# A fused decoder kernel: the second key stage recorded in written order, its rotations put behind the next product's addition, and layer 0's rows loaded sooner and taken ahead of the context

## The chip, the core and the metric

The kernel is one launch on one core of a Trainium2 chip. A core has a matrix engine (TensorE, PE in the profile), a vector engine (VectorE, DVE), an activation engine (ScalarE, ACT), a general engine (GpSimd, POOL) and a synchronising engine (SyncE, SP) that here only issues DMA transfers. Each engine takes the instructions of its own queue; semaphores order the engines among each other. The metric is device time in microseconds for one execution; lower is better.

## The reference, cut to what matters

Two batches of 512 rows of width 1024 pass through four residual layers; a context of 1024 rows per batch feeds the first and the third.

```python
x = x + matmul(fake_quant(layernorm(x)), fake_quant(ctx))           # layer 0 "xattn"
x = x + linear(layernorm(x)) + lora(...)                            # layer 0 "ffn"
x = x + attention(layernorm(x), ctx, ctx, mask, wq, wk, wv, wo)     # layer 1, rotated q and k
x = x + linear(layernorm(x)) + lora(...)                            # layer 1 "ffn"
# fake_quant: q = clip(round(x / scale + zp), 0, 255); (q - zp) * scale
# rope: x * cos + rotate_half(x) * sin
```

The keys `k = rope(ctx @ wk)` and the values `v = ctx @ wv` of layer 1 depend on the context alone, so the kernel makes them first; layer 0 is done beside them.

## The kernel before, in words

**Products.** Keys, values, queries and linear layers are multiplied in float32 as 2 by 2 blocks with seven products in place of eight. `seven` runs the products in the order 1, 2, 6, 7, 5, 4, 3. Its accumulators are the four PSUM banks of tag `b`; products 1 and 2 share a bank, 7 and 4, 5 and 3. A product that adds onto a shared bank can't begin until the earlier content has been read: product 4 waits for the addition L281, which reads product 7's bank, and product 3 waits for L283, which reads product 5's. Four products of 512 columns in 128-partition pieces make one `seven` product: eight matmul records of the trace, 3.4 to 3.5 us.

**Operands.** `right_steps` forms four sums of context blocks (L247, L250, L252, L255, each 128x2048) and `left_steps` four sums of weight blocks (L233, L236, L238, L241, each 128x1024), all on VectorE. Products 6, 7, 5, 4, 3 need them.

**Stages.** Keys come in two stages (`keys(0, 0, ...)` and `keys(0, 1, ...)`), each of two groups m = 0, 1 of seven products; then two value stages; then the same for batch 1. When a key block is complete, `emit` rotates it: `rope` calls `rope_steps`, two ScalarE copies of 64 partitions (L204, L205) and three VectorE operations (L207, L210, L211), and SP stores the result. In the first stage the order of TensorE, VectorE and ScalarE is the written one (`manual_schedule`). In the second stage and all that follows up to the attention, only TensorE keeps the written order; VectorE's and ScalarE's is made by a planner.

**Layer 0.** `quantized_product(b)` is a generator that `weave` advances once in two product steps. It first quantizes the eight blocks of context rows (L414 loads each, L182, L185, L186 quantize), then normalizes and quantizes four blocks of rows (`layernorm`, L151 to L156, then `quantized`), turns each on TensorE (L424), copies it out (`copy_out`, L144 on ScalarE and L146 on VectorE in turn), sums it (L427), and multiplies (L447, L461). The rows of batch 0 are loaded behind the first stage on ScalarE's DMA queue (L1119). Small operations on the quantization parameters (L1122 to L1126, `qp`) are written behind the first stage; the planner places them.

**Queues.** SP issues in order: the first weights and context blocks, rotation tables, the four quantization parameters (L1066), router weights (L1069) and gate weights (L1070); then key stores, later weights and context rows as they come.

**Attention.** A head's `exponential(j)` adds the negated maximum on VectorE (L809), takes the exponential on ScalarE (L812) and sums on GpSimd. While the first heads are filled in, the loop at L917 runs the last query products between them and calls `place_maximum` and `exponential` for the first head.

Of the kernel before, what the change touches and what calls it, by code (L numbers as in the profile page):

```python
# [39 lines left out]
def decoder_kernel(  # L40
# [139 lines left out]
    def quantized(dst, src, side):  # L180

        nc.vector.tensor_scalar(  # L182
            src, src, qp[f"{side}_inv"], qp[f"{side}_zp"], ALU.mult, ALU.add
        )
        nc.vector.tensor_scalar(src, src, 0.0, QMAX, ALU.max, ALU.min)  # L185
        nc.vector.tensor_scalar(dst, src, RND, RND + QMID, ALU.add, ALU.subtract)  # L186
# [6 lines left out]
        nc.scalar.copy(dsts[0], tr[:, 0:4, :])  # L193
        nc.vector.tensor_copy(dsts[1], tr[:, 4:8, :])

    def rope(dst, acc, half, scale):

        for _ in rope_steps(dst, acc, half, scale, nc.vector):
            pass

    def rope_steps(dst, acc, half, scale, eng):

        rot = u2([P, HALF])
        nc.scalar.activation(rot[0:64, :], acc[64:128, :], AF.Copy, scale=scale)  # L204
# [167 lines left out]
    def rows(b, t):  # L372
        return x[b][t // 2][:, t % 2, :]

    def halves():
        return [u8([P, 2, D]) for _ in range(2)]
# [30 lines left out]
        return right_sums(nc.vector, *quarters, lambda: u8([P, 4, HALF]))  # L407


    def quantized_product(b):  # L410
        q2 = [u8([P, 4, D], BF16) for _ in range(2)]
        for k in range(NKT):
            c_t = u4([P, D])
            nc.sync.dma_start(c_t, ctx_in[b, ts(k, P), :])  # L414
            quantized(q2[k // 4][:, k % 4, :], c_t, "x2")
            if k % 2:
                yield
        x1T = u8([P, NC, S], BF16)
        rsum, l1s = [], []

        def turned(t):
            tr = ps_wide().bitcast(BF16)[:, 0 : NC * P].rearrange("p (c n) -> p c n", c=NC)
            for c in range(NC):
                nc.tensor.transpose(tr[:, c, :], l1s[t][:, ts(c, P)], ident_b)  # L424
            copy_out(x1T[:, :, ts(t, P)], tr)
            r = small([P, 1])
            nc.scalar.activation(u4([P, D]), l1s[t], AF.Copy, accum_out=r)  # L427
            nc.vector.tensor_scalar(r, r, c_x2, None, ALU.mult)
            rsum.append(r)

        for t in range(NT):
            h = layernorm(rows(b, t))
            l1 = u2([P, D], BF16)
            quantized(l1, h, "x1")
            l1s.append(l1)
            if t > 1:
                turned(t - 2)
            yield
        turned(NT - 2)
        yield  # L440
        turned(NT - 1)
# [12 lines left out]
        csum = u4([P, D])  # L454
        nc.vector.tensor_scalar(csum, cs, kc2, c_x1, ALU.add, ALU.mult)
        yield
        for t in range(NT):
            acc = ps_wide()
            for n in range(2):
                for c in range(NC):  # L460
                    nc.tensor.matmul(  # L461
                        acc[:, ts(n, HALF)],
                        x1T[:, c, ts(t, P)],
                        q2[c // 4][:, c % 4, ts(n, HALF)],
                        start=(c == 0),
                        stop=(c == NC - 1),
                    )
            y = u4([P, D])
            nc.vector.scalar_tensor_tensor(y, acc, rsum[t], csum, ALU.add, ALU.add)
            xs = rows(b, t)  # L470
            nc.vector.scalar_tensor_tensor(xs, y, s12, xs, ALU.mult, ALU.add)
            yield


    def keys(b, q, ctx_ops, w, begun=(None, None)):
        def group(m):
            def product(i, acc, start):
                accumulate(
                    acc,
                    [(w[i - 1][:, c, ts(m, P)], ctx_ops[i - 1][:, c, :]) for c in range(4)],  # L480
                    start,
                )

            def emit(i, j, src):
                dst = u2([P, HALF]) if (i, j) == (0, 0) else src
                rope(dst, src, j, 1.0)
                nc.sync.dma_start(kT_d[b][4 * q + 2 * i + m][:, ts(j, HALF)], dst)

            return seven(product, emit, begun[m])

        return group(0), group(1)
# [359 lines left out]
    def attention(extra):  # L851
# [28 lines left out]
        for n in range(-2, total + GRP + 1):  # L880
# [36 lines left out]
            for i in range(extra.pop(n, 0)):  # L917
                for _ in range(2):
                    next(tree, None)
                next(extra["products"])  # L920

                if mid and not old and i == 1:
                    mid.place_maximum()
                    mid.exponential(0)
                if mid and not old and i == 2:
                    mid.exponential(1)
            if n == GRP:
                w_ops = {i: output_operand(0, i) for i in (1, 6, 2, 7, 5, 4, 3)}
            for _ in tree:
# [138 lines left out]
    nc.sync.dma_start(eb_t, ebias.partition_broadcast(P))  # L1068
    nc.sync.dma_start(r0_t, r0T.rearrange("(c p) e -> p c e", p=P))  # L1069
    nc.sync.dma_start(ga_t, gaT.rearrange("(c p) e -> p c e", p=P))  # L1070


    ctx_ops = [ctx_raw[0], ctx_raw[2]] + [None] * 5
# [2 lines left out]

    for i in range(20):
        nc.tensor.matmul(begun[0][:, :P], ones_b, ones_b, start=True, stop=True)
    first = [keys(0, 0, ctx_ops, w[0], begun), keys(0, 1, ctx_ops, w[1])]

    def layer_0():
        yield from quantized_product(0)
        put_away(0)
        x[1] = halves()
        load_rows(1, nc.sync)
        yield from quantized_product(1)

    with tc.manual_schedule(engines={mybir.EngineType.DVE, mybir.EngineType.Activation}):
# [13 lines left out]
        for g in first[0]:  # L1102
            next(g)
        next(first[0][0])
        next(rights)
        next(lefts)
        next(first[0][1])
        w[0][:] = next(lefts)
        ctx_ops[:] = next(rights)
        for _ in range(2):  # L1110
            for g in first[1]:
                next(g)
        lefts = left_steps(nc.vector, *wk_raw[1], lambda: u4([P, 4, 256]))
        for i, _ in enumerate(chain(*first[0])):
            if i in (4, 5, 6, 7):
                w[1][:] = next(lefts) or w[1]

        x[0] = halves()
        load_rows(0, nc.scalar)  # L1119

    for side in ("x1", "x2"):
        nc.vector.reciprocal(qp[f"{side}_inv"], qp[f"{side}_scale"])  # L1122
    for c_t, side in ((c_x1, "x1"), (c_x2, "x2")):
        nc.vector.tensor_scalar(c_t, qp[f"{side}_zp"], -1.0, QMID, ALU.mult, ALU.add)
# [3 lines left out]
    side = layer_0()  # L1128
    for b in range(B):
        if b == 1:  # L1130
            for ch in range(2):
# [3 lines left out]
        for i, stage in enumerate((keys, keys, values, values)):  # L1135
# [6 lines left out]
            if (b, i) == (0, 1):  # L1142
                main = chain(*first[1])
                raw = raw_weights(wv, 0)
                weave(main, side, 2)
                w = quad_sums(raw)
            else:
                main = pair(*stage(b, i % 2, ctx_ops, w))
                weave(main, side, 2)
                if i < 3:  # L1150
                    w = quad_weights((wk, wv)[(i + 1) // 2], (i + 1) % 2)
# [280 lines left out]
```

## Time and profile before

| What | us |
|---|---|
| median of 3 runs (lowest, highest) | 2435.92 (2434.83, 2436.45) |
| profiled execution, its own time | 2434.64 |
| its span | 2432.8 |
| TensorE busy | 2407.8 (99%) |
| VectorE busy | 1842.8 (76%) |
| GpSimd busy | 1024.5 (42%) |
| ScalarE busy | 527.2 (22%) |

Time is read in us from the start of the span. A bracket behind a row of the timeline names the idle time before it and what ended it. The stages that the diff touches lie in the first 205 us; one more edit lies near 955 us. In this trace TensorE starts the first key product at 3.92, the second key stage's remaining products after 68, the value products at about 111, and layer 0's products of batch 0 (L461) at 161.2.

### The profile page before, as it was taken

The numbers are of one execution on the slowest core, as the hardware profiler recorded it, in microseconds if no ns is written. First come the engines' busy times: TensorE is split into PE (matmuls) and PEld (weight loads), VectorE is DVE, ScalarE is ACT, GpSimd is POOL, SyncE is SP. The second block draws the span as 40 slices with busy tenths as digits, with TensorE's granted clock in tenths as the row PEclk, the third lists the DMA queues.
The fourth block names the chain that finished last, engine by engine and source line by source line (L and its number), as shares of the span: only waits on it lengthen the run. The fifth ranks groups of instructions, "written<-read, shape, count | busy, mean of one in ns | idle before, by whom it ended". The sixth has DMA issues, their size and how long they took to land.

```text
span 2432.8 us, 19529 instructions
## 1 busy us (share of the span) xinstructions
PE 2407.8 (99%) x6792; PEld 1195.1 (49%) x6792; DVE 1842.8 (76%) x1998; ACT 527.2 (22%) x623; POOL 1024.5 (42%) x543
## 2 busy tenths in 40 slices
PE   9999999999999999999999999999999999999999
PEld 4477458654444444444444444444444444444444
DVE  5849774345986556898888888888898988888753
ACT  1210221011222222322222222222223222222210
POOL 0000010210000002777676767667776767677531
PEclk9999999999999999999999999999999999999999
DMA  5437133013796221344223323442332243233501
GB/s 197 169 99 281 70 131 112 26 61 116 280 334 212 78 90 53 101 141 117 75 80 106 117 68 89 143 143 79 129 117 78 95 123 116 66 91 109 173 9 61
DMA packets 151506, 288.01 MB, mean 118 GB/s; under 512 B 32112, under 2 KB 49776, under 8 KB 149104
## 3 DMA queue, kind: packets, MB, share of 16 engines
q1 hardware_dynamic: 110880, 244.54, 30.6%
q10 hardware_dynamic: 40384, 41.70, 5.6%
q8 instruction: 54, 0.88, 0.1%
q0 software_dynamic: 144, 0.52, 0.1%
q14 instruction: 44, 0.36, 0.1%
HBM read 223.54 MB, written 63.18 MB: 118 GB/s over the span
## 4 chain that ended last, share of the span: by engine, by line
PE 55%; DVE 4%; issue 1%; POOL 0%; ACT 0%; POOLq 0%; DVEq 0%; ACTq 0%
PE b L345 20%; PE wide L763 16%; PE b L826 16%; PE wide L727 2%; DVE u L809 1%; DVE u L777 0%; DVE u L789 0%; DVE small L729 0%; DVE u L318 0%; DVE u L787 0%; PE b L967 0%; PE wide L192 0%; DVE u L791 0%; DVE u L785 0%; PE wide L1016 0%
## 5 line engine op out<-in xcount | busy, mean ns | idle before, releaser
L345 PE MATMUL b<-u,u 128*128 128x512 f32 (+1 forms) x3600 | 1384.5, 541 | 14.8 <-DVE u L283 4.2
L345 PEld LDWEIGHTS b<-u,u 128*128 128x128 f32 x3600 | 681.3, 191 | 684.0 <-issue 605.2
L826 PE MATMUL b<-u,u 128*128 128x512 f32 x1024 | 460.3, 592 | 0.0
L763 PE MATMUL wide<-u,u 128*128 128x512 f32 x1024 | 452.6, 593 | 2.6 <-DVE u L777 1.7
L815 POOL TENSOR_TENSOR u<-u 128x1024 f32<-128x1024 f32 x64 | 151.6, 2368 | 705.3 <-ACT u L812 696.8
L777 DVE TENSOR_TENSOR u<-wide,u 128x1024 f32<-128x1024 f32 x256 | 312.7, 1223 | 125.3 <-PE wide L763 125.1
L812 ACT ACTIVATE u<-u 128x2048 f32<-128x2048 f32 x128 | 244.7, 1911 | 665.1 <-DVE u L809 662.3
L763 PEld LDWEIGHTS wide<-u,u 128*128 128x128 f32 x1024 | 192.8, 190 | 250.9 <-issue 175.5
L809 DVE TENSOR_TENSOR u<-u,b 128x2048 f32<-128x2048 f32 x128 | 290.1, 2267 | 3.0 <-ACT b L805 3.0
L826 PEld LDWEIGHTS b<-u,u 128*128 128x128 f32 x1024 | 186.2, 192 | 184.6 <-issue 184.6
L300 POOL TENSOR_TENSOR u<-u,u 128x512 f32<-128x512 f32 x120 | 184.3, 1562 | 170.3 <-DVE u L312 134.6
L318 DVE TENSOR_TENSOR u<-u,b 128x512 f32<-128x512 f32 x200 | 135.6, 679 | 121.7 <-PE b L345 114.4
L818 POOL TENSOR_TENSOR u<-u,u 128x1024 f32<-128x1024 f32 x64 | 150.7, 2355 | 30.9 <-ACT u L812 30.7
L819 POOL TENSOR_TENSOR u<-u,u 128x1024 f32<-128x1024 f32 x64 | 150.8, 2356 | 5.0
L204 ACT ACTIVATE u<-u 64x512 f32<-64x512 f32 x72 | 45.2, 628 | 361.6 <-DVE u L283 162.5
L837 POOL TENSOR_TENSOR u<-u,u 128x512 f32<-128x512 f32 x64 | 115.0, 1797 | 18.4 <-DMA u<-row 18.4
L785 DVE TENSOR_TENSOR u<-u 128x1024 f32<-128x1024 f32 x64 | 113.0, 1765 | 0.0
L727 PEld LDWEIGHTS wide<-ident,u 128*128 128x128 f32 x512 | 79.9, 203 | 61.8 <-issue 55.7
L605 POOL TENSOR_TENSOR u<-u,u 128x1024 f32<-128x1024 f32 x8 | 20.2, 2528 | 213.0 <-DVE u L156 210.4
L787 DVE TENSOR_TENSOR u<-u,u 128x1024 f32<-128x1024 f32 x64 | 107.5, 1679 | 0.2
L820 POOL TENSOR_TENSOR u<-u 128x512 f32<-128x512 f32 x64 | 100.1, 1564 | 5.0
L1158 POOL DMA_DIRECT2D u<-in_b_dram x1 | 0.7, 717 | 229.1 <-PE b L345 229.1
(136 smaller groups left out, 1639.4 us busy)
## 6 DMA issues: line engine op xcount, KB each, us to landing
u<-row ACTq DMA_DIRECT2D x128, 256.0 KB, 3.5
u<-wo SPq DMA_DIRECT2D x64, 512.0 KB, 4.3
u<-in_wo_dram SPq DMA_DIRECT2D x48, 512.0 KB, 4.4
u<-in_wq_dram SPq DMA_DIRECT2D x32, 512.0 KB, 4.3
q<-u SPq DMA_DIRECT2D x64, 256.0 KB, 2.3
u<-in_wo_dram SPq DMA_DIRECT2D x16, 1024.0 KB, 8.0
wo<-u SPq DMA_DIRECT2D x32, 512.0 KB, 4.4
u<-q SPq DMA_DIRECT2D x64, 256.0 KB, 4.5
```

The costliest lines, as they stand in the source:

```text
L300: nc.gpsimd.tensor_tensor(c, c, what, ALU.add)
L318: nc.vector.tensor_tensor(c, c, acc, ALU.add)
L345: nc.tensor.matmul(acc, lhsT, rhs, start=start and k == 0, stop=k == len(pairs) - 1, skip_group_check=True,)
L727: nc.tensor.transpose(tr[:, t, :], src[:, t, :], ident)
L763: nc.tensor.matmul(sc[:, ts(n, HALF)], self.kT[:, ts(2 * j + n, P)], self.qT, start=True, stop=True,)
L777: nc.vector.tensor_tensor(self.e[j // 2][:, js, :], sc.rearrange("p (k q) -> p k q", k=2), mask[j], ALU.add)
L809: nc.vector.tensor_tensor(e, e, self.nmf.unsqueeze(1).to_broadcast([P, 4, S]), ALU.add)
L812: nc.scalar.activation(e, e, AF.Exp)
L815: nc.gpsimd.tensor_tensor(d, e[:, 0:2, :], e[:, 2:4, :], ALU.add)
L818: nc.gpsimd.tensor_tensor(d, d, e[:, 0:2, :], ALU.add)
L819: nc.gpsimd.tensor_tensor(d, d, e[:, 2:4, :], ALU.add)
L826: nc.tensor.matmul(self.acc, self.v[:, k, :], self.e[j][:, k % 4, :], start=(k == 0), stop=(k == NKT - 1),)
```

## The change

- `rope` is gone; `keys` gets an argument `later`. A rotation's ScalarE copies are still issued with the block, but its three VectorE operations and the store are put on a list when `later` is given, and run one product step afterwards.
- The second key stage is recorded under `manual_schedule` for VectorE and ScalarE, so their written order holds there.
- `quantized_product(b, rows_first)`: for batch 0 the rows now come before the context. All four blocks' moments, one square root for the four and one reciprocal come in a step of their own, taken within the first stage (at step 8 of its last loop).
- The rows of batch 0 are loaded on SP's queue directly behind the gate weights, in place of ScalarE's queue after the first stage.
- In the fill-in of the attention the first head's two exponentials come one product later each (i = 2 and 3 in place of 1 and 2).

```diff
-    def rope(dst, acc, half, scale):
-        for _ in rope_steps(dst, acc, half, scale, nc.vector):
-            pass
...
+    def quantized_product(b, rows_first=False):
+        q2, x1T, rsum, l1s = [], [], [], []
+        def quantized_context():
...
+        def quantized_rows():
+            x1T.append(u8([P, NC, S], BF16))
+            mv, rstd = small([P, NT, 2]), small([P, NT])
+            if rows_first:
+                for t in range(NT):
+                    moments(rows(b, t), mv[:, t, :])
+                nc.scalar.activation(rstd, mv[:, :, 1], AF.Sqrt, bias=eps_t)
+                nc.vector.reciprocal(rstd, rstd)
+                yield
+            for t in range(NT):
+                if rows_first:
+                    h = scaled(rows(b, t), mv[:, t, 0:1], rstd[:, t : t + 1])
+                else:
+                    h = layernorm(rows(b, t))
+                l1 = u2([P, D], BF16)
+                quantized(l1, h, "x1")
+                l1s.append(l1)
+                if t > 1:
+                    turned(t - 2)
+                yield
...
+        parts = [quantized_context, quantized_rows]
+        for part in reversed(parts) if rows_first else parts:
+            yield from part()
...
-    def keys(b, q, ctx_ops, w, begun=(None, None)):
+    def keys(b, q, ctx_ops, w, begun=(None, None), later=None):
...
+            def finish(i, j, src):
+                dst = u2([P, HALF]) if (i, j) == (0, 0) else src
+                yield from rope_steps(dst, src, j, 1.0, nc.vector)
+                nc.sync.dma_start(kT_d[b][4 * q + 2 * i + m][:, ts(j, HALF)], dst)
             def emit(i, j, src):
-                dst = u2([P, HALF]) if (i, j) == (0, 0) else src
-                rope(dst, src, j, 1.0)
-                nc.sync.dma_start(kT_d[b][4 * q + 2 * i + m][:, ts(j, HALF)], dst)
+                steps = finish(i, j, src)
+                next(steps)
+                if later is None:
+                    next(steps, None)
+                else:
+                    later.append(steps)
...
                     mid.place_maximum()
-                    mid.exponential(0)
-                if mid and not old and i == 2:
-                    mid.exponential(1)
+                if mid and not old and i > 1:
+                    mid.exponential(i - 2)
...
     nc.sync.dma_start(ga_t, gaT.rearrange("(c p) e -> p c e", p=P))
+    x[0] = halves()
+    load_rows(0, nc.sync)
...
+    later = []
+    first = [keys(0, 0, ctx_ops, w[0], begun), keys(0, 1, ctx_ops, w[1], later=later)]
     def layer_0():
-        yield from quantized_product(0)
+        yield from quantized_product(0, True)
...
+        for rotation in later:
+            next(rotation, None)
+        later.clear()
...
         for i, _ in enumerate(chain(*first[0])):
             if i in (4, 5, 6, 7):
                 w[1][:] = next(lefts) or w[1]
-        x[0] = halves()
-        load_rows(0, nc.scalar)
+            if i == 8:
+                next(side)
...
-                weave(main, side, 2)
+                with tc.manual_schedule(
+                    engines={mybir.EngineType.DVE, mybir.EngineType.Activation}
+                ):
+                    due = []
+                    for k, _ in enumerate(main):
+                        for rotation in due:
+                            next(rotation, None)
+                        due = later[:]
+                        later.clear()
+                        if k % 2 == 0:
+                            next(side)
+                    for rotation in due:
+                        next(rotation, None)
                 w = quad_sums(raw)
```

More of the change, by code (lines that the diff above doesn't have):

```diff
@@ L407, in context_sums @@
         return right_sums(nc.vector, *quarters, lambda: u8([P, 4, HALF]))
[L410 to L419, printed above, removed]
+    def quantized_product(b, rows_first=False):
+        q2, x1T, rsum, l1s = [], [], [], []
+        def quantized_context():
+            q2.extend(u8([P, 4, D], BF16) for _ in range(2))
+            for k in range(NKT):
+                c_t = u4([P, D])
+                nc.sync.dma_start(c_t, ctx_in[b, ts(k, P), :])
+                quantized(q2[k // 4][:, k % 4, :], c_t, "x2")
+                if k % 2:
+                    yield
         def turned(t):
@@ L424, in turned @@
                 nc.tensor.transpose(tr[:, c, :], l1s[t][:, ts(c, P)], ident_b)
-            copy_out(x1T[:, :, ts(t, P)], tr)
+            copy_out(x1T[0][:, :, ts(t, P)], tr)
             r = small([P, 1])
@@ L429, in turned @@
             rsum.append(r)
[L431 to L437, printed above, removed]
+        def quantized_rows():
[17 more added lines that the diff above has]
+                    turned(t - 2)
+                yield
+            turned(NT - 2)
             yield
-        turned(NT - 2)
-        yield
-        turned(NT - 1)
+            turned(NT - 1)
+        parts = [quantized_context, quantized_rows]
+        for part in reversed(parts) if rows_first else parts:
+            yield from part()
         cs = ps_wide()
@@ L462, in quantized_product @@
                         acc[:, ts(n, HALF)],
-                        x1T[:, c, ts(t, P)],
+                        x1T[0][:, c, ts(t, P)],
                         q2[c // 4][:, c % 4, ts(n, HALF)],
@@ L1078, in decoder_kernel @@
         nc.tensor.matmul(begun[0][:, :P], ones_b, ones_b, start=True, stop=True)
-    first = [keys(0, 0, ctx_ops, w[0], begun), keys(0, 1, ctx_ops, w[1])]
+    later = []
+    first = [keys(0, 0, ctx_ops, w[0], begun), keys(0, 1, ctx_ops, w[1], later=later)]
     def layer_0():
-        yield from quantized_product(0)
+        yield from quantized_product(0, True)
         put_away(0)
@@ L1086, in layer_0 @@
         yield from quantized_product(1)
+    side = layer_0()
     with tc.manual_schedule(engines={mybir.EngineType.DVE, mybir.EngineType.Activation}):
@@ L1116, in decoder_kernel @@
                 w[1][:] = next(lefts) or w[1]
-        x[0] = halves()
-        load_rows(0, nc.scalar)
[L1121 to L1124, printed above, removed]
+            if i == 8:
+                next(side)
+    for of in ("x1", "x2"):
+        nc.vector.reciprocal(qp[f"{of}_inv"], qp[f"{of}_scale"])
+    for c_t, of in ((c_x1, "x1"), (c_x2, "x2")):
+        nc.vector.tensor_scalar(c_t, qp[f"{of}_zp"], -1.0, QMID, ALU.mult, ALU.add)
     nc.vector.tensor_scalar_mul(kc2, c_x2, float(D))
     nc.vector.tensor_tensor(s12, qp["x1_scale"], qp["x2_scale"], ALU.mult)
-    side = layer_0()
     for b in range(B):
```

## Prediction

> **What bounds the kernel now.** I read the page first, then TensorE's timeline, its waits, its clock in 1 us stretches, and VectorE's timeline below 140 us.
>
> ```profile
> PE 2407.8 (99%) x6792; PEld 1195.1 (49%) x6792; DVE 1842.8 (76%) x1998; ACT 527.2 (22%) x623; POOL 1024.5 (42%) x543
> ```
>
> TensorE sets the end, so an edit is worth only what it adds to or takes from TensorE's gaps. Its timeline shows where they are (start, length, group, idle before it):
>
> ```profile
> 44.60 38.03 PE L345 MATMUL b<-u,u 128*128 128x512 f32 x88 [0.49 <-DVE u L281]
> 86.09 15.70 PE L345 MATMUL b<-u,u 128*128 128x512 f32 x32 [3.45 <-DVE u L283]
> 102.80 3.70 PE L345 MATMUL b<-u,u 128*128 128x512 f32 x8 [1.02 <-DVE u L281]
> 107.25 14.06 PE L345 MATMUL b<-u,u 128*128 128x512 f32 x56 [0.75 <-DVE u L283]
> ...
> 125.88 9.69 PE L345 MATMUL b<-u,u 128*128 128x256 f32 x32 [4.11 <-ACT u L274]
> ```
>
> Four gaps, 3.45 + 1.02 + 0.75 + 4.11 = 9.33, lie in the second key stage and the start of the values. The two long ones also cost clock. The stretches' tenth column is the granted clock:
>
> ```profile
> 85.00:86.00 1.00, 0.00 (x0) 0.00 (x0) 1.00 (x3) 0.00 (x0) 0.00 (x0) 1.00 1.02 418
> 86.00:87.00 1.00, 0.91 (x2) 0.62 (x3) 1.00 (x3) 0.87 (x2) 0.00 (x0) 0.81 1.02 414
> 87.00:88.00 1.00, 1.00 (x2) 0.34 (x1) 1.00 (x3) 0.39 (x1) 0.00 (x0) 0.50 1.04 414
> ...
> 90.00:91.00 1.00, 1.00 (x4) 0.50 (x3) 1.00 (x3) 0.00 (x0) 0.00 (x0) 0.98 0.11 37
> ```
>
> Clock 0.5 from about 86.6 to 90.0. The 32 records take 15.70 where 32 at the rate of the row of 88 (38.03 / 88 = 0.432) take 13.8: 1.9 lost. After the gap of 4.11 the clock is 0.5 up to 131.0; 32 records of 256 columns take 9.69 where the next such row takes 7.12: 2.6 lost. So all that this stage can give back is 9.33 + 1.9 + 2.6 = 13.8.
>
> Check: from the start of product 4 of the second stage's first group (82.63 - 3.46 = 79.17) to the first layer-0 product (161.2) are 7 key products (24.0), 4 turns (1.8), 11 value products (39.2) and the column sums (3.45), 68.5 in all; the trace takes 82.0, so 13.5 is lost. I use 13.5.
>
> **The change part by part.**
>
> *The small operations move to the head of VectorE's queue.* The diff doesn't say this; the built program's order does. In the kernel before, VectorE goes from `ident_b` to L247, L250, and meets the first reciprocal (L1122) six operations behind L247. In the changed kernel all six parameter operations stand in front of L247. They wait for the four parameter loads, the last four of some 20 on SP before the router weights:
>
> ```profile
> 20.00 2.29 DVE L247 TENSOR_TENSOR u<-u,u 128x2048 f32<-128x2048 f32 x1 [18.07 <-DMA u<-in_ctxT_in_dram]
> 23.96 2.29 DVE L250 TENSOR_TENSOR u<-u,u 128x2048 f32<-128x2048 f32 x1 [1.67 <-DMA u<-in_ctxT_in_dram]
> ...
> 29.77 0.16 DVE L1122 RECIPROCAL qp_x_inv<-qp_x_scale 128x1 f32<-128x1 f32 x1
> ...
> 43.86 0.69 DVE L281 TENSOR_TENSOR u<-u,b 128x512 f32<-128x512 f32 x1
> ```
>
> ```profile
> L1066 SPq DMA_DIRECT2D qp_x_zp<-in_x_zp_dram x2: 328/328/328, 19.9 to 23.9; - x2
> ...
> DMA to landing us min/median/max: 4.6/6.5/8.3
> ```
>
> The second zero point is issued at 23.9 and lands 4.6 later, 28.5; the other three land at 28.0 to 28.4 by their own rows. SP's order up to there is unchanged, so I keep these times. Behind them: c_x2 and kc2 0.25, then L247 at 28.8 in place of 20.0; L250 at 31.1 (waiting for nothing else); L233 at 33.3 in place of 26.17: 7.1 late. The small operations no longer stand in between (0.12 + 0.13 + 0.14), so L281 ends at 51.3, not 44.55. From 24 to 46 VectorE has no idle time, so nothing absorbs it. TensorE had 4.4 us of slack at product 6 and none at product 4 (the 0.49 above). It waits at products 6 (33.6 to 36.4: needs the weight sum and the bank that L207 reads), 7 (1.6), 5 (1.7) and 4 (1.2): 7.3 against 0.49. Product 4 starts at 51.3: 6.7 late.
>
> A rule speaks against it too: the Trainium skill (TensorE: Matmul & The Clock Gate, engine queue depths) calls VectorE a strict FIFO. The trace has its instance: L182 waits for a context row until 84.63, ready L283 stands behind it, and TensorE idles 3.45 for L283. If VectorE could pass waiting operations, this term would be 0; I take FIFO.
>
> *The row step in the first stage.* The rotations of the first stage are not deferred; VectorE reaches the end of the block before L290 at 71.24 + 6.7 = 77.9. There now stand four moments (8 statistics of 0.60, 4 aggregates of 0.2 to 0.3) and one addition: 6.3, to 84.2. Then the reciprocal waits for ScalarE: a table load and the root, 82.12 to 83.82 in this trace, 1.7: 86.0. Behind it, ahead of product 4's addition L281: reciprocal 0.1, L290 0.6, row 0's L156 and L182 0.72 each, L185 and L186 0.6 each, the last rotation 1.8, L281 itself 0.7: 5.9, to 91.9. TensorE has run 10 products since 51.3 (34.6) and stands from 85.9: a new wait of 6.0. Product 4 starts at 91.9 in place of 79.2: 12.7 late. Both waits are VectorE's chain, so a half clock inside them costs nothing.
>
> *Clock after that wait.* Rows: 1.9 and 2.6. Rule, same page, What's actually happening: half rate after an idle window of about 3.4 us, full again after one busy window, windows free-running. That means 3.4 to 6.8 at half rate, 1.7 to 3.4. I take 2.1 (0.9 to 3.4). The page would not throttle for the wait of 2.8 in the first stage; the row after 121.76 throttled with 2.4 idle; either way VectorE hides it.
>
> *What goes.* With the rows first, nothing that needs a context row stands before the second stage's additions, and the rotations stand behind them. In the order, the additions of the second group follow TensorE by one block of row work (2.7 for L156, L182, L185, L186) plus one rotation (1.8), under two products of 3.43. I count no further gap up to the values: all 13.5 goes. Cover: some 2 us of VectorE idle before its additions; without it each late addition costs its own delay. The wait for L274 (4.11) goes with it, since ScalarE's copy now stands before the row sums of later rows.
>
> *Row loads on SP.* Four more issues of about 0.4 at 28 to 30. Behind them is the first key store, which waits for VectorE anyway (36 or later). 2 MB land by about 36, where DMA was 0 to 0.5 busy; they are first read at 77.9. Cost 0.
>
> *Context rows later.* They now load from about 122 to 134, behind key and value stores, and the last three meet ScalarE's two context blocks of 1 MB each. VectorE takes them in the value stage, where L182 of the sixth and seventh row stands ahead of an L281 that TensorE wants at about 10 us after their issue. Before, loads in such company took:
>
> ```profile
> L414 SPq DMA_DIRECT2D u<-in_ctx_in_dram x6: 430/624/1243, 200.2 to 204.2; - x6
> ...
> DMA to landing us min/median/max: 6.2/7.1/10.6
> ```
>
> There the two 1 MB blocks landed after 10.6 and 13.0, so the rows went first. 7 to 8, plus 2.6 of VectorE, is about TensorE's time: 0.3 (0 to 3.9).
>
> *Fill-in of the attention.* Before, product 6 waits 1.25 at 957.99 because L278 stands behind L809. Now L278 is first: 0.65 saved. But the second L809 and the maximum's reduction (L729) move behind the next addition; two score products wait for their PSUM buffers, 1.3 and 0.6 (0 to 2.2 together). Net +1.0 (-0.65 to +1.5), half-way to the upper end by counting each operation at its row.
>
> Sum: 12.7 + 2.1 - 13.5 + 0.3 + 1.0 = +2.6 against the profiled 2434.64 (span 2432.8 and 1.8 around it): 2437.2. The median is 1.3 above the profiled time: **2438.5**.
>
> **Rivals.** A: a second long wait in the values. Place: L182 of the sixth context row (about 140 us). If ScalarE's 2 MB go first, the row lands 9 to 10 after issue, TensorE waits 3.9 and the clock halves again, 2.0. It decides once that row lands more than about 7.5 after its issue. For it: rows in company of row loads took 7.7 to 10.0 at 72 to 82. Against: the row above. Price 5.6 more: +8, 2444.
>
> B: the head of the queue is free earlier, because parameter loads land with the context (24) or VectorE isn't held. Then product 4 starts 12.7 - 6.7 = 6.0 late: -4.1, 2431.8. For it: the reciprocals showed no wait at 29.77. Against: their landing rows, which don't depend on VectorE.
>
> C: the edits gain nothing: one more gap like the old 3.45 with its clock remains among the second group's additions. +2.6 + 5.3 = +8. For it: VectorE is above 95% busy from 86 to 120 now. Against: the work there is less by eight context rows (8 x 2.0).
>
> **How the numbers follow.** 0.2% is 4.9 us, about what a measurement tells from no change. Main case 0.58, its own range -0.5 to +5.5 (clock ±1.3, wait ±1, attention ±1), 2435.4 to 2441.4: 0.52 within, 0.05 slower, 0.01 faster. A 0.17 and C 0.10: nearly all slower (0.23), 0.04 within. B 0.15: 0.07 faster, 0.08 within. Together 0.08 faster, 0.64 same, 0.28 slower. The range 2432.0 to 2445.0 leaves out about half of B and a tail of A and C.
>
> **What would show it.** TensorE waits for VectorE at products 6, 7, 5, 4 between 33 and 52; L247's successor starts at 28 to 29 with the parameter loads as releaser; one wait of 5 to 6.5 near 86 to 92 by the addition of product 7, with clock 0.5 after it; no gap over 1 from 95 to 140; two small waits of the scores near 965. Wrong if VectorE starts by 25, if the wait near 86 is under 3, or if a gap over 2 stands behind 95.

## The result and the profile after

The changed kernel takes 2447.84 (median of 6 runs, 2444.14 to 2448.45) against 2436.18 for the kernel before beside it: ratio 1.0041, 95% interval 1.0030 to 1.0051. A second measurement gives 2445.99 (5 runs, ratio 1.0039, 1.0027 to 1.0052). The median of the eleven is 2446.3, and experiments are compared with that. The forecast was 2438.5 within 2432 to 2445 and most likely no change; the kernel is some 10 us slower.

The profiled execution took 2447.89 with a span of 2446.1, 13.3 above the span before. TensorE's timeline of the changed kernel (start, length, group, idle before it and what ended it):

```profile
36.67 3.70 PE L341 MATMUL b<-u,u 128*128 128x512 f32 x8 [2.67 <-DVE u L203]
...
51.84 34.60 PE L341 MATMUL b<-u,u 128*128 128x512 f32 x80 [0.94 <-DVE u L277]
92.33 9.58 PE L341 MATMUL b<-u,u 128*128 128x512 f32 x16 [5.89 <-DVE u L277]
...
124.32 20.94 PE L341 MATMUL b<-u,u 128*128 128x256 f32 x96
148.86 8.66 PE L341 MATMUL b<-u,u 128*128 128x256 f32 x32 [3.60 <-DVE u L277]
157.57 3.40 PE L460 MATMUL wide<-u,ones_b 128*128 128x512 bf16 x15
160.81 7.07 PE L341 MATMUL b<-u,u 128*128 128x256 f32 x32
167.72 3.62 PE L474 MATMUL wide<-u,u 128*128 128x512 bf16 x15
```

The reader is to see three things. Product 4 of the second stage's first group starts at 92.33 behind a wait of 5.89, in place of 79.17. The four old gaps between 83 and 126 are gone. A wait that was not there before, 3.60, stands at 148.86, in the value products.

VectorE's timeline explains the first. Its queue stands still until the parameter loads have landed, and before the addition L277 it works through the moments, the root, and the first row:

```profile
28.21 0.16 DVE L1149 RECIPROCAL qp_x_inv<-qp_x_scale 128x1 f32<-128x1 f32 x1 [26.28 <-DMA qp_x_scale<-in_x_scale_dram]
...
29.01 2.28 DVE L243 TENSOR_TENSOR u<-u,u 128x2048 f32<-128x2048 f32 x1
...
84.43 0.21 DVE L152 BATCH_NORM_AGGREGATE small<-small 128x2 f32<-128x12 f32 x1
86.34 0.18 DVE L435 RECIPROCAL small<-small 128x4 f32<-128x4 f32 x1 [1.71 <-ACT small L434]
...
91.59 0.68 DVE L277 TENSOR_TENSOR u<-u,b 128x512 f32<-128x512 f32 x1
```

The stretches of 1 us show what the wait costs beyond its length. The third figure from the end is the granted clock: half from about 90.5 to 97.3.

```profile
90.00:91.00 1.00, 0.00 (x0) 0.00 (x0) 1.00 (x3) 0.00 (x0) 0.00 (x0) 0.73 0.00 0
91.00:92.00 1.00, 0.00 (x0) 0.00 (x0) 1.00 (x3) 0.00 (x0) 0.00 (x0) 0.50 0.06 20
...
97.00:98.00 1.00, 1.00 (x3) 0.40 (x3) 0.00 (x0) 0.00 (x0) 0.00 (x0) 0.85 0.00 0
```

The 16 records behind the wait take 9.58 where 16 at 0.432 take 6.9: 2.7 lost.

The new wait at 148.86 begins on the queues. SyncE issues the context rows, ScalarE the two 1 MB blocks of the next context (columns as above; a queue's own issue time):

```profile
132.92 0.33 SPq L413 DMA_DIRECT2D u<-in_ctx_in_dram  x1
135.59 0.33 SPq L533 DMA_DIRECT2D v<-u  x1
136.02 1.98 SPq L413 DMA_DIRECT2D u<-in_ctx_in_dram  x3
```

```profile
135.01 0.93 ACTq L396 DMA_DIRECT2D u<-in_ctxT_in_dram  x2
```

```profile
144.77 0.81 DVE L182 TENSOR_SCALAR u<-u,qp_x_inv,qp_x_zp 128x1024 f32<-128x1024 f32 x1 [3.99 <-DMA u<-in_ctx_in_dram]
...
148.12 0.68 DVE L277 TENSOR_TENSOR u<-u,b 128x512 f32<-128x512 f32 x1
```

The sixth row is issued at 136.02, behind a value store, and 1.0 after ScalarE's blocks. VectorE gets it at 144.77, 8.75 later. L277 stands behind it in the queue, and so do the end of the fifth row, the rest of the sixth and the start of the seventh: L277 ends at 148.80, 4.03 after the landing. TensorE has stood since 145.26, 9.24 after the row's issue.

The attention's lines:

```profile
968.05 3.70 PE L341 MATMUL b<-u,u 128*128 128x512 f32 x8 [0.85 <-DVE u L274]
...
975.33 1.98 PE L785 MATMUL wide<-u,u 128*128 128x512 f32 x4 [1.39 <-DVE small L751]
977.65 3.70 PE L785 MATMUL wide<-u,u 128*128 128x512 f32 x8 [0.34 <-DVE u L799]
...
1000.12 3.70 PE L785 MATMUL wide<-u,u 128*128 128x512 f32 x8 [0.66 <-DVE u L799]
```

The wait at product 6 falls from 1.25 to 0.85; the two score waits that were forecast are there, and a third, at 1000.12.

The whole difference between the two profiled executions, by start times of the same work in both:

| Place | Forecast | Traces |
|---|---|---|
| product 4 starts later (79.17 to 92.33) | +12.7 | +13.2 |
| half clock behind that wait | +2.1 | +2.7 |
| old gaps and their clock | -13.5 | -14.6 |
| wait in the values, its half clock, rest | +0.3 | +5.4 |
| first layer-0 product (161.03 to 167.72) | +1.6 | +6.7 |
| from there to the attention (924.46 to 934.91 in all) | 0 | +3.8 |
| attention's fill-in (990.48 to 1003.66 in all) | +1.0 | +2.7 |
| sum | +2.6 | +13.2 |

The third and fourth rows use the work between product 4 and the first layer-0 product: 7 key products at 3.43, 4 turns at 0.445, 11 value products at 3.455 and 3.45 of column sums, 67.25. Before, the stretch took 81.86, so 14.6 was lost; after, 75.39, so 8.1, of which 2.7 is the first row's clock. The other 5.4 are the wait of 3.6, 1.6 of half clock (8.66 where the next such row takes 7.07) and 0.2 that no row shows.

The +3.8 is the one entry that the medians contradict: 2446.3 - 2436.2 is 10.1, not 13.3. In the query stage, 600 to 925, TensorE waited 0.7 for VectorE in the profiled execution of before and 3.3 in that of after. The order of every engine in that stage is the same in both kernels. Runs e4, e5 and e10 below bear on this.

### The profile page after: what moved, and what is told of

The parts are those of the page before. It is cut to its first block, busy times and chain, and to the rows that moved or that the text cites. A ratio compares the mean times of both kernels' runs of the same rounds, so it can differ in the third digit from the quotient of the medians.

```text
span 2446.1 us, 19508 instructions
## 1 busy us (share of the span) xinstructions
PE 2409.5 (99%) x6784; PEld 1194.0 (49%) x6792; DVE 1843.5 (75%) x1995; ACT 526.2 (22%) x620; POOL 1026.5 (42%) x543
## 4 chain that ended last, share of the span: by engine, by line
PE 61%; DVE 5%; issue 1%; POOL 1%; DMA 1%; ACT 0%; SPq 0%; POOLq 0%; DVEq 0%; ACTq 0%
PE b L341 27%; PE wide L785 16%; PE b L848 16%; PE wide L749 2%; DVE u L831 2%; DMA u<-in_wo_dram 1%; DVE small L751 0%; DVE u L799 0%; DVE u L811 0%; DVE u L314 0%; DVE u L809 0%; DVE u L203 0%; PE b L988 0%; PE wide L192 0%; POOL u L840 0%
```

## The experiments

The theory after the result: three losses, each with a place of its own (parameters at the head of VectorE's queue; the row step in front of L277; the sixth context row beside ScalarE's blocks) and a fourth in the attention, against a gain that comes from the rows standing first. The rival is that VectorE has the same work anyway, so that every wait only moves. The eleven runs of the changed kernel spread over 4.3, so a difference of 2 to 4 between medians is read only together with the waits in the trace.

**e1: the parameter operations late.** The six operations leave the head of the queue.

```
+    def parameters():
+        for of in ("x1", "x2"):
+            nc.vector.reciprocal(qp[f"{of}_inv"], qp[f"{of}_scale"])
...
             if i == 8:
+                parameters()
                 next(side)
-
-    for of in ("x1", "x2"):
-        nc.vector.reciprocal(qp[f"{of}_inv"], qp[f"{of}_scale"])
...
```

> The changed kernel, but the six parameter operations stand behind the first stage's rotations, directly ahead of the row moments, so that the first context difference does not wait for them. Theory (VectorE is held at the head of its queue, and the wait of the second stage is VectorE's chain, which moves with it): the first difference starts at 20.0 in place of 29.0, the waits at products 6, 7, 5 of the first stage (5.8 in all) go, product 4 of the second stage's first group starts about 85 in place of 92.3, still after a wait of 6 to 6.5, and the time is 6 to 7.5 lower than the changed kernel's 2447.8. Rival (the second wait ends by something of fixed time, such as the landing of the rows): product 4 still starts near 92, the wait is 12, the time is within 1 of the changed kernel. Second rival: the sixth context row is no earlier by the clock, so that its wait in the values grows by what was gained ahead of it, and the gain is under 3.

Measured: 2439.42 (20 runs; ratio to before 1.0014, 1.0007 to 1.0020), 6.9 below the changed kernel. TensorE's timeline of e1:

```profile
85.37 9.78 PE L341 MATMUL b<-u,u 128*128 128x512 f32 x16 [6.39 <-DVE u L277]
142.66 10.17 PE L341 MATMUL b<-u,u 128*128 128x256 f32 x32 [4.15 <-DVE u L277]
```

The waits at products 6, 7 and 5 of the first stage are gone, product 4 starts 7.0 earlier, and the wait in front of it moved along with VectorE's chain. The first rival is out, and so is the second by its own measure, a gain under 3. In the profiled execution the wait in the values did grow, to 4.15 with 3.1 of half clock, which gives back 2.1 of the 7.0; but that execution was the slowest of the 20 (2443.79), and the median does not show this loss.

**e2: the context blocks behind the rows.**

```
-                    ctx_raw[2 * ch] = context_quarter(1, ch, 0, nc.scalar)
+                    ctx_raw[2 * ch] = context_quarter(1, ch, 0, nc.sync)
```

> The changed kernel, but the two 1 MB context blocks of the next batch are issued by SP directly behind the last context row, not by ScalarE ahead of the sixth. Theory (the sixth row lands late since ScalarE's 2 MB go first): it lands within 5 of its issue in place of 8.7, the wait of 3.6 at 148.9 and the half clock behind it (1.6) go, and the time is 4.5 to 5.5 lower than the changed kernel's. Rival (the row is late because SP issues it only behind a value store that waits for ScalarE): the wait stays above 2 and the time is within 2 of the changed kernel.

Measured: 2442.88 (7 runs; ratio 1.0028, 1.0017 to 1.0038), 3.4 below the changed kernel. SyncE's and VectorE's lines, then TensorE's, of e2:

```profile
136.21 1.35 SPq L413 DMA_DIRECT2D u<-in_ctx_in_dram  x3
137.61 1.34 SPq L396 DMA_DIRECT2D u<-in_ctxT_in_dram  x2
```

```profile
142.73 0.81 DVE L182 TENSOR_SCALAR u<-u,qp_x_inv,qp_x_zp 128x1024 f32<-128x1024 f32 x1 [2.19 <-DMA u<-in_ctx_in_dram]
```

```profile
146.72 7.17 PE L341 MATMUL b<-u,u 128*128 128x256 f32 x32 [1.26 <-DVE u L277]
```

With the blocks behind it, the row is there 6.5 after its issue in place of 8.75, the wait falls from 3.60 to 1.26, and no half clock follows (7.17 for 32 records). So ScalarE's blocks made about two thirds of the wait. Neither expectation was met: the row did not land within 5 and the gain is below 4.5 to 5.5, but the wait is also below the rival's 2. What is left of the wait comes from the row's late issue behind the value store and from the 3.9 of VectorE's work between its landing and the end of L277.

**e3: the attention back.** The exponentials stand one step earlier again, as in the kernel before.

```
                     mid.place_maximum()
-                if mid and not old and i > 1:
-                    mid.exponential(i - 2)
+                    mid.exponential(0)
+                if mid and not old and i == 2:
+                    mid.exponential(1)
```

> The changed kernel, but both exponentials of the middle head stand where they stood before, behind product 2 and product 6 (first and second step) in place of the second and third. Theory (the two score waits of 1.39 and 0.34 near 975 and that of 0.66 at 1000 come from the exponential standing behind the next addition): they go, the wait at product 6 is 1.25 again, the time is 2.0 to 2.8 lower than the changed kernel's. Rival (the wait moves to another place of the attention, since VectorE has the same work): within 0.7 of it.

Measured: 2444.09 (5 runs; ratio 1.0035, 1.0021 to 1.0049), 2.2 below. In its trace none of the waits of 1.39, 0.34 and 0.66 is left, and product 6 waits 1.25 again:

```profile
967.44 3.70 PE L341 MATMUL b<-u,u 128*128 128x512 f32 x8 [1.25 <-DVE u L274]
```

The five runs overlap those of the changed kernel; that the 2.2 are the edit's rests on these waits and on e10, whose interval is clear of no change.

**e10: the same edit alone, in the kernel before.** (Where the text below says "behind products 6 and 2 in place of 2 and 6 wait", it means that each exponential stands one step later, behind the second and third step in place of the first and second.)

> The kernel before with the exponentials behind products 6 and 2 in place of 2 and 6 wait, that is one step later each, and nothing else of the change. Theory: it costs here what taking it back gained, 2 to 2.8 above the kernel before, by waits of 1.4, 0.3 and 0.7 at 965, 967 and 990 against 0.4 saved at 957. Rival (the cost comes from where the attention stands in the changed kernel): within 1 of it. Its query stage between 600 and 930 is a third look at the order before.

Measured: 2439.08 (20 runs) against 2436.48, ratio 1.0011 (1.0004 to 1.0017), 2.6 above. Its trace has the same three waits as the changed kernel:

```profile
969.47 1.98 PE L763 MATMUL wide<-u,u 128*128 128x512 f32 x4 [1.39 <-DVE small L729]
...
994.26 3.70 PE L763 MATMUL wide<-u,u 128*128 128x512 f32 x8 [0.66 <-DVE u L777]
```

So this edit costs 2.2 to 2.7 in both kernels; in e10 nothing else of the change is there.

**e4 and e5: the two kernels once more, unchanged.** They are about the +3.8 of the query stage.

> The changed kernel once more. Theory for the 3.9 that it loses between 640 and 770 (the first load of output weights at 624 took 2.1 to issue and started 3.4 after it, because a code fetch of SP fell beside a query store; every later load of this queue is then late): it is a matter of the single execution. Times should fall at 2444 and at 2448; an execution at 2444 shows that load issued in under 1 and no waits at 648, 684, 747, one at 2448 shows both. Rival (the loss is the order's own): every execution has it, and the two times differ elsewhere.

> The kernel before once more, for its waits between 600 and 930. Theory (the changed kernels' waits there, 1.8 to 4.1 in every profile, are not the order's, since the order of all engines in this stage is the same in both kernels; they follow the landing of the first load of output weights, 6.4 after issue before, 8 to 9 in the changed ones): a second execution of the kernel before can have them too, 1.5 or more where that load lands after 8. Rival (something of the changed kernels that lasts, such as what its queues still carry, makes them): again under 1.0 and a landing of about 6.4.

Measured: e4 2445.99 (2444.46 to 2447.39, spread evenly, not at two times), e5 2437.62. In e4 the first load of output weights was issued in 0.73, not 2.10, and TensorE still waited 2.8 in the query stage. So the slow issue is not the cause; that part of the theory is wrong. e5 shows that the kernel before has such waits too (TensorE's line of e5):

```profile
664.71 14.00 PE L345 MATMUL b<-u,u 128*128 128x512 f32 x32 [2.03 <-DVE u L283]
```

Summed over 600 to 925 the waits for VectorE and ScalarE are 0.7 (before), 3.9 (before again), 3.6 (e10, the order of before there), 3.3 (after), 2.8 (after again), and 1.8 to 4.7 in the other kernels. The profiled execution of before was the exception, and the +3.8 is not put down to the change. e5's largest wait of VectorE there is 2.57 for a load of output weights at 643, not for the first one, which landed after 6.8, so a late first load is not the common cause either: the theory's landing after 8 was not met, and the waits were there. What makes these loads late in one execution and not in another is open.

**e6: the three mends together.** e1, e2 and e3 in one kernel, and as a fourth edit each context row issued two rows ahead of its quantization, so that it is not queued behind the value store:

```
+            c_ts = []
-            for k in range(NKT):
-                c_t = u4([P, D])
-                nc.sync.dma_start(c_t, ctx_in[b, ts(k, P), :])
-                quantized(q2[k // 4][:, k % 4, :], c_t, "x2")
+            for k in range(NKT + 2):
+                if k < NKT:
+                    c_ts.append(u4([P, D]))
+                    nc.sync.dma_start(c_ts[k], ctx_in[b, ts(k, P), :])
+                k -= 2
+                if k < 0:
+                    continue
+                quantized(q2[k // 4][:, k % 4, :], c_ts[k], "x2")
```

> The changed kernel with the parameter operations late (as in e1), the next batch's two context blocks on SP behind the context rows (as in e2) and each context row issued two rows ahead of its quantization, and the exponentials back (as in e3). Theory (the three losses are separate and add): no wait above 1 in the values up to the first layer-0 product, none of the score waits, only the wait of 6.4 at 85 left with its half clock; from e1's 2439.4 that takes the values' 4.15 and 3.1 of clock and the attention's 2.7: 2429 to 2432. Rival (they hide one another, the query stage between 600 and 930 takes back what comes early): above 2434.

Measured: 2431.0 (8 runs; ratio 0.9978, 0.9968 to 0.9988). TensorE's timeline of e6:

```profile
85.77 8.84 PE L341 MATMUL b<-u,u 128*128 128x512 f32 x16 [6.38 <-DVE u L277]
...
117.01 28.05 PE L341 MATMUL b<-u,u 128*128 128x256 f32 x128
```

The value products run through without a wait, and what is left is the wait of the row step. The time is 15.3 below the changed kernel, where 14.3 to 17.3 were expected. So the losses do not hide one another: e1, e2 and e3 gained 6.9, 3.4 and 2.2 one by one, 12.5 together. The fourth edit, meant for what e2 left of the wait, was not run alone.

**e7: the row step taken apart.** e6, and the moments one by one between the first stage's weight sums, each row's work one step later:

```
                 for t in range(NT):
                     moments(rows(b, t), mv[:, t, :])
+                    yield
                 nc.scalar.activation(rstd, mv[:, :, 1], AF.Sqrt, bias=eps_t)
-                nc.vector.reciprocal(rstd, rstd)
                 yield
+                nc.vector.reciprocal(rstd, rstd)
...
+            if i in (3, 4, 5, 6, 8):
+                next(side)
             if i == 8:
                 parameters()
-                next(side)
...
-                        if k % 2 == 0:
+                        if k % 2:
                             next(side)
```

> The kernel of e6, and in it the four row moments stand one by one behind steps 3 to 6 of the first stage (between its weight sums), the root behind step 8, and each row's work behind the second and every other addition of the second stage in place of the first. Theory (the wait of 6.4 comes from the place of the step, not from the work): it falls to waits of about 2.8 at 64 and 0.4 at 99 with less half clock, 4.5 to 6 below e6, 2424 to 2427. Rival (VectorE is full from 24 to 120 whatever the order, so the wait only moves): within 1.5 of e6.

Measured: 2426.6 (5 runs; ratio 0.9962, 0.9949 to 0.9974), 4.4 below e6 and the fastest of all: 9.9 below the kernel before. TensorE's timeline of e7:

```profile
64.82 29.36 PE L341 MATMUL b<-u,u 128*128 128x512 f32 x64 [2.59 <-DVE u L277]
...
113.40 28.16 PE L341 MATMUL b<-u,u 128*128 128x256 f32 x128
```

One wait of 2.59 takes the place of 6.38, and none above 0.3 follows up to the row at 113.40. That difference, 3.8, is most of the gain; at the first layer-0 product e7 is 3.5 ahead of e6. VectorE's work is the same; its place made the wait. The pauses of 1.3 to 1.4 in which VectorE waits for each rotation's copies are as many as in e6; what is gone from its queue is the wait of 1.70 for the root, which now runs while VectorE does other work.

**e8 and e9: which half of the change removed the old gaps.** e8 is the changed kernel with the rotations at once; e9 is e1 with the context rows first.

```
-    first = [keys(0, 0, ctx_ops, w[0], begun), keys(0, 1, ctx_ops, w[1], later=later)]
+    first = [keys(0, 0, ctx_ops, w[0], begun), keys(0, 1, ctx_ops, w[1])]
```

> The changed kernel with the second key stage's rotations done at once again; the rows stay ahead of the context. Theory (the old gaps of 13.5 went because nothing that needs a context row stands before the additions; the deferral only saves short waits): waits of 1.5 and 0.4 near 111 and 115, 1 to 3 above the changed kernel. Rival (the deferral is what removed the gaps): 6 or more above it.

```
-        yield from quantized_product(0, True)
+        yield from quantized_product(0)
```

> The kernel of e1 with the context rows ahead of layer 0's rows as in the kernel before; rotations still behind the next product's addition. Theory: the old gaps come back in the second group (3.4 near 109, 3.8 near 124) with some 4 of half clock, and the wait of the values (4.15 and 3.1 of clock) goes: 3 to 6 above e1, 2442.5 to 2445.5. Rival (the deferral of the rotations removed the gaps): 5 or more below e1.

Measured: e8 2442.6 (15 runs; ratio 1.0025, 1.0018 to 1.0033), 3.7 below the changed kernel; e9 2446.92 (4 runs; ratio 1.0043, 1.0029 to 1.0057), 7.5 above e1. TensorE's timeline of e9:

```profile
112.03 7.15 PE L341 MATMUL b<-u,u 128*128 128x512 f32 x24 [3.35 <-DVE u L279]
...
126.68 5.41 PE L341 MATMUL b<-u,u 128*128 128x256 f32 x16 [3.54 <-ACT u L270]
```

With the context first two long gaps are back, although the rotations are still deferred; with the rows first they stay away, although the rotations are done at once. So it was not the deferral that removed them but the rows' place. The recorded reason for that, an addition behind a context row that has not landed, is not what e9 shows: from 72 to 132 no VectorE operation waits for a load. Its lines show row 0's moments and their root in front of the addition, 3.2 from 104.83 to 108.06:

```profile
106.15 0.21 DVE L152 BATCH_NORM_AGGREGATE small<-small 128x2 f32<-128x12 f32 x1
108.06 0.16 DVE L164 RECIPROCAL small<-small 128x1 f32<-128x1 f32 x1 [1.70 <-ACT small L163]
...
111.29 0.68 DVE L279 TENSOR_TENSOR u<-u,b 128x512 f32<-128x512 f32 x1
```

With the context first, each row's moments and root stand in the second stage again; with the rows first they are taken together in the first stage. In the kernel before, the gap of 3.45 was a context row's, as the prediction read it, but the copy L274 that ended the gap of 4.11 stood behind a root as well (ScalarE's lines):

```profile
124.81 0.29 ACT L163 ACTIVATE small<-small,eps_one 128x1 f32<-128x1 f32 x1 [1.75 <-DVE small L152]
125.24 0.58 ACT L274 COPY u<-b 128x512 f32<-128x512 f32 x1
```

No run takes the later context rows and the earlier moments apart. e9's excess over the 3 to 6 expected is, in its profiled execution, in later waits (1.35 for a weight load at 186.69, and 2.73 with half clock in place of 1.51 near 350).

e8 missed both its theories: it is faster than the changed kernel. Its key stage shows only 0.24 of new idle time, at 116.3. The gain lies in the values; TensorE's, VectorE's, SyncE's and ScalarE's lines of e8:

```profile
145.78 7.17 PE L341 MATMUL b<-u,u 128*128 128x256 f32 x32 [0.78 <-DVE u L277]
```

```profile
143.12 0.81 DVE L182 TENSOR_SCALAR u<-u,qp_x_inv,qp_x_zp 128x1024 f32<-128x1024 f32 x1 [0.20 <-DMA u<-in_ctx_in_dram]
...
145.05 0.68 DVE L277 TENSOR_TENSOR u<-u,b 128x512 f32<-128x512 f32 x1
```

```profile
135.71 2.10 SPq L413 DMA_DIRECT2D u<-in_ctx_in_dram  x3
```

```profile
136.03 1.76 ACTq L396 DMA_DIRECT2D u<-in_ctxT_in_dram  x2
```

Two things differ from the changed kernel. The sixth row was issued 0.3 ahead of ScalarE's blocks, not 1.0 behind them, and was there after 7.4. And the planner put less in front of the addition: 2.6 from the landing to the end of L277, not 4.0. The wait of 3.60 with its half clock shrank to 0.78 without. VectorE's shorter way, 1.4, is half of that; how much the order of the two issues gave is not shown, since with ScalarE's blocks 1.0 ahead the landing itself came after 7.96 (e4) to 9.27 (e1).

**e11: the rotations at once in e7.** If the deferral were worthless, it should be so here too.

> The kernel of e7 with the second key stage's rotations done at once again. Theory (in e8 the deferral was worth nothing only because the wait of 5.9 in front let VectorE catch up; here VectorE has no such slack, and four instructions of a rotation, 1.8 to 2.5, stand ahead of an addition that TensorE wants): waits of about 4 near 103 and 1.8 near 120 with some half clock, 6 to 9 above e7, 2432 to 2436. Rival (the deferral gives nothing, as e8 seems to say): within 1.5 of e7's 2426.6.

Measured: 2434.83 (13 runs; ratio 0.9986, 0.9978 to 0.9994, against 0.9962 for e7: 0.24% or 5.9 more, just under the 6 to 9 expected). TensorE's timeline of e11:

```profile
103.57 8.83 PE L341 MATMUL b<-u,u 128*128 128x512 f32 x16 [3.59 <-DVE u L277]
...
139.34 7.17 PE L341 MATMUL b<-u,u 128*128 128x256 f32 x32 [1.75 <-DVE u L277]
```

The rival is out. In e7 the deferral is worth some 6 us; in the changed kernel it is worth nothing. The recorded reason, that VectorE catches up during the wait of 5.9, fits the traces. In e8 row 0's work and a rotation stand in front of the first L277 of the second stage, inside that wait, and two rows and three rotations between it and the next (91.45 to 111.25); in e11 three rows and four rotations stand there (78.47 to 102.84). But e7 also moved the rows' work by one addition, so the reason is argued and not tested alone.

## Why the prediction was wrong, point by point

*The parameter operations* (6.7): right. L243 starts at 29.0 (forecast 28.8), TensorE waits at products 6, 7, 5 and 4, product 4 starts at 51.84 (51.3). e1 gives back 7.0 at product 4 of the second stage and 6.9 of the time. VectorE as a strict queue held.

*The row step* (6.0): right. Wait 5.89 forecast as 6.0, and e7 shows that it was the step's place. It need not be the rows' work: in e9 context rows stand there, and TensorE waits 6.41 at the same product (85.50). *Clock behind it* (2.1): 2.7, inside 0.9 to 3.4.

*What goes* (13.5): all of it went, as forecast; the size was 14.6, since the 11 value products were counted at 39.2 where 11 at 3.455 are 38.0 (and the first layer-0 product starts at 161.03, not 161.2). The reason given was half right. e9 and e8 say that it was the rows' place, while the deferred rotations added nothing in this kernel. And the wait of 4.11 was put down to row sums in front of L274, where a root stood that waited for a row's moments.

*Context rows later* (0.3, 0 to 3.9): this step failed, in all three terms of its sum. It took a landing of 7 to 8 and 2.6 of VectorE's work against TensorE's time, about 10 after the row's issue. The profile after shows 8.75 and 4.03 against 9.24, which makes the wait of 3.6. The largest error, 1.4, is VectorE's work: 2.6 is about what the sixth row and L277 take, and the end of the fifth row and the seventh row's L182 stand there too. The landing is 1.25 above the middle of its range, and TensorE wants the addition 0.8 sooner. In e4, the same kernel once more, the row landed after 7.96, inside the range, and the wait with its half clock (8.86 for 32 records) was still there:

```profile
148.02 8.86 PE L341 MATMUL b<-u,u 128*128 128x256 f32 x32 [2.81 <-DVE u L277]
```

Rival A had the place, the wait (3.9 forecast, 3.6 measured) and the half clock (2.0; 1.6), but not what decides: it asked for a landing above 7.5, and with 4.03 and 9.24 the addition is late for any landing above 5.2; e2's row landed after 6.5 and left 1.26. That A's price fits so well is in part luck. The evidence for A was in hand, rows that had taken 7.7 to 10.0 at 72 to 82, and it got 0.17. The main case looked at loads at 200 to 204, where the rows had been issued first; the order in time of the two issues in the new kernel was not worked out: ScalarE's issue came together with its copy of a value product at 134.98, SyncE's sixth row behind the store that waits for the end of that copy (135.59). The main case's upper end of 3.9 also left out the half clock. The prediction's own sign of being wrong, a gap over 2 behind 95, is this wait.

*Fill-in of the attention* (+1.0, at most 1.5): too small, 2.7. The waits of 1.3 and 0.6 were forecast and came as 1.4 and 0.3. A third, 0.66 at 1000.12, was not looked for, since the step followed the edit through one group of products only, and product 6 saved 0.4 in place of 0.65.

*The sum*: the two failed terms are 5.1 + 1.7 of the miss of 7.8 (2446.3 - 2438.5); the clock's 0.6 and product 4's 0.5 are offset by 1.1 more from the gaps, and 1.0 stays unassigned within the spread of the runs. A's price alone would have given 2444; the attention put the time beyond the range. B and C are out: VectorE was held until 28.2, and no gap stands between 95 and 145.

## What to carry to other kernels

When two queues start large transfers at about the same time, work out from the order of both queues which issue comes first, and price the reader behind the loser with its half clock: here putting two blocks behind the rows was worth 3.4 (e2). Then count every operation that the reader's engine does between the landing and the one that is waited for; the two that were left out here took about 1.4. Look at every instruction that a planner puts ahead of the first one on an engine; six of 0.15 us cost 7, because they waited for loads. And one profiled execution can be the odd one: a difference in a stage whose order did not change is to be looked at in a second execution of both kernels before it is explained.

## What the runs showed of the hardware that was not expected

The half clock does not follow the length of a wait. At one place, with the same work around it, a wait of 3.45 halved the clock in the kernel before and left it full in e10, where the 32 records behind it take 14.00 and not 15.70:

```profile
86.03 14.00 PE L345 MATMUL b<-u,u 128*128 128x512 f32 x32 [3.45 <-DVE u L283]
```

In e2 a wait of 2.07 was enough:

```profile
36.41 8.96 PE L341 MATMUL b<-u,u 128*128 128x512 f32 x16 [2.07 <-DVE u L203]
```

```profile
37.00:38.00 1.00, 1.00 (x2) 0.34 (x1) 1.00 (x2) 0.00 (x0) 0.00 (x0) 0.50 0.06 16
```

Between these two lengths both outcomes occur: in e7 a wait of 2.59 (at 64.82) halved the clock, in the changed kernel one of 2.67 (at 36.67) did not. Every wait of 3.5 or more in the traces halved it. The half clock lasted about 3.4 or 6.8, partly inside the wait, and cost 1.6 behind 3.60 in the changed kernel, 3.1 behind 4.15 in e1. The Trainium skill (TensorE: Matmul & The Clock Gate, What's actually happening) puts the half clock behind at least one idle window of about 3.4, with free-running windows. Free-running windows fit the scatter; the bound does not, as 2.07 was enough. For a wait between 2.0 and 3.5 both outcomes have to stand in the range, 0 and a cost of up to about 3.

A context row of 512 KB was there 6.5 after its issue where 2 MB came behind it on the same queue (e2), 7.4 where the 2 MB were issued on the other queue 0.3 after it (e8), and 8.0 to 9.3 where they were issued there 1.0 ahead of it (after, e1, e3, e4). And the query stage, with one order of all instructions, waited 0.7 and 3.9 in two executions of the kernel before.
